# Adjacency pieces loaded from ScalarE's queue into one buffer more, with another split between two stages

## The chip, the cores and the metric

The kernel runs on one core of a Trainium2 chip. The metric is the device time in microseconds (us) of one execution. The profiles show five engines: TensorE (PE in the profile, with its weight loads as PEld), VectorE (DVE), ScalarE (ACT), GpSimd (POOL) and SyncE (SP). SP has no computation in these profiles; what it does there is issue transfers. ACT and POOL issue transfers too, between their other instructions: the load of one piece took 0.33 us to issue on SP, and 0.56 us on POOL in the kernel before. A profile is of one execution, and its span leaves out some 2 us of that execution's time, so spans of one profile and medians of several runs differ slightly. When a transfer lands is read from the profile; times to landing count from its issue.

## The reference, cut to what matters

Two layers on 4096 nodes with 512 features. The adjacency `adj` is 4096 x 4096, mostly zero.

```python
# layer 0
xw = max(sign(x), 0) @ sign(weight0).T
x  = layernorm(x + relu(adj @ xw))
# layer 1
h = x @ edge_w
e = where(adj > 0, h @ h.T, NEG_BIG)
edge_att = softmax(e, axis=1);  node_att = softmax(x @ node_w, axis=0)
x = layernorm(x + adj * (node_att * edge_att) @ (x @ weight1) + bias)
```

Layer 1 needs `adj > 0` as a mask. The kernel makes part of that mask early and in a smaller form: it loads 80 pieces of `adj` (128 rows x 1024 columns, 512 KB each), turns each into a bf16 mask on VectorE, and stores the mask (256 KB) to memory. That work has nothing to do with layer 0 or with the product h. It is only put beside them, to use their idle engines and transfer time.

## The kernel before

In layer 0, each block of 128 nodes takes 64 matmuls: the adjacency block `at` comes in two halves, each half is worked in two quarters, and each quarter is split into a high part (`hi`, a cast on ScalarE) and the rest (`lo`, a subtraction on VectorE). Both have two buffers. `premask` is called once per half.

```python
bufs = deque([pair[:, 0, :], pair[:, 1, :], single])
loaded = deque()

def premask(queue, left):
    if loaded and (len(bufs) == 1 or len(pieces) == left):
        (r, j, c), a = loaded.popleft()
        m = ...                                   # a, seen as bf16; a_ is a in the same shape
        tc.keep_in_program_order(nc.vector.tensor_scalar(m, a_, 0.0, NEG_BIG, ALU.is_le, ALU.mult))
        nc.gpsimd.dma_start(mask_d[r][:, c : c + 2, j, :], m)       # store the mask
        bufs.append(a)
    if len(pieces) > left:
        r, j, c = pieces.popleft()
        a = bufs.popleft()
        queue.dma_start(a, adj[ts(r * BG + j, P), c * W : (c + 2) * W])   # load a piece
        loaded.append(((r, j, c), a))

def aggregate(b):
    ...
    for half in range(2):
        at = stream.tile(...)                     # three buffers
        nc.sync.dma_start(at, adj_t[b, :, ts(half, HB), :])
        for q in range(2):
            ...                                   # aq: a quarter of at; tiles hi and lo, two buffers each
            nc.scalar.copy(hi, aq)
            nc.vector.tensor_sub(lo, aq, hi.bitcast(F32))
            if q == 0:
                premask(nc.gpsimd, 40)
            for c in range(QC):
                nc.tensor.matmul(acc, hi[:, c, :], xw[:, kb, :], ...)
                nc.tensor.matmul(acc, lo[:, c, :], xw[:, kb, :], ...)
    ...                                           # normalisation, rows stored
```

`tc` is a framework that orders the instructions of each engine by simulating the program, and puts in the waits. An instruction may come earlier in its engine's queue than it is written, as soon as the simulation has its inputs ready and its buffer free. `tc.keep_in_program_order(i)` forbids that for `i`: it stays behind all that was written before it for the same engine. The kernel uses it for the mask operation.

Other duties of GpSimd in layer 0: for each block, `left` and the row additions (`sums_l`, `scr`) and their stores. In the stage h (the product with `edge_w`, 56 steps of 1.72 us of matmul work) `premask(nc.sync, 0)` is called at every step after the sixth, with five buffers. The node softmax needs two reductions over partitions on GpSimd (`gmax`, `gsum`); they are written after h.

## Time and profile before

| | before |
|---|---|
| time, median of 3 | 2092.13 us (2091.34 to 2095.67) |
| layer 0 ends, h starts | 593.4 us |
| h (to the first matmul after it) | 127.2 us |
| all that follows | 1373.4 us |
| PE busy, idle from 58 to 593 | 478.4 us, 56.6 us |

The stage borders are the first starts of the matmuls of h and of the stage after it. The last row is the view by windows; the columns after the length are the busy us (and instructions) of PE, PEld, DVE, ACT and POOL, the granted clock of PE (as the profile gives it, 1.00 being its full speed), the share of time the DMA engines were busy, and GB/s:

```profile
58.00:593.00 535.00, 478.39 (x2049) 387.23 (x2048) 311.58 (x379) 148.37 (x181) 217.80 (x267) 0.95 0.68 234
```

The longest waits of GpSimd in layer 0, at loads for stored masks (total us, times, longest us):

```profile
POOL pair L274 <- DMA mask_d<-pair: 144.9, 25, 10.4
POOL single L274 <- DMA mask_d<-single: 70.5, 12, 10.0
```

### The profile page before, as it was taken

The page shows a single profiled execution, that of the slowest core. Times are in us where ns is not written, and L with a number is a line of the kernel's source. Part 1 is how long each engine was busy: PE and PEld are TensorE (multiplying, and loading weights), DVE is VectorE, ACT ScalarE, POOL GpSimd, SP SyncE. Part 2 cuts the span into 40 slices and gives each one's busy share as a digit, 9 for nine tenths or more (in the row PEclk, how much of TensorE's full clock was granted, in tenths as well). Part 3 has the DMA queues.
Part 4 walks back from the last instruction along what each step waited for, and adds up shares of the span by engine and source line. Part 5 has one row for each costly group of instructions (what it writes and reads, how often), then busy time and mean ns, then how long its engine had stood idle before and what let it go on. Part 6 is the DMA issues. An engine that isn't in the chain of part 4 may idle for free.

```text
span 2094.0 us, 18051 instructions
## 1 busy us (share of the span) xinstructions
PE 1990.7 (95%) x6108; PEld 1104.9 (53%) x6108; DVE 1377.1 (66%) x1896; ACT 673.0 (32%) x1107; POOL 526.4 (25%) x643
## 2 busy tenths in 40 slices
PE   8998887889997899999999899999999999999998
PEld 6786666678852344545555444444444444444443
DVE  7665555555566546656746877696669686887724
ACT  5332222223320156857657641112112211221100
POOL 0433433343443211111102211151114311240101
PEclk9998998999999999999999999999999999999999
DMA  8776676676537847857859897667667756766431
GB/s 298 279 271 234 210 266 218 220 286 209 195 116 274 307 173 272 316 186 262 288 205 346 297 337 259 235 241 262 230 218 264 253 195 230 265 243 222 162 107 60
DMA packets 133643, 497.70 MB, mean 238 GB/s; under 512 B 14000, under 2 KB 14000, under 8 KB 125872
## 3 DMA queue, kind: packets, MB, share of 16 engines
q0 software_dynamic: 77248, 283.15, 36.9%
q1 hardware_dynamic: 55728, 212.36, 30.2%
q10 hardware_dynamic: 576, 1.05, 0.1%
q8 instruction: 48, 0.79, 0.1%
q14 instruction: 43, 0.35, 0.0%
HBM read 376.96 MB, written 119.54 MB: 237 GB/s over the span
## 4 chain that ended last, share of the span: by engine, by line
PE 70%; DMA 14%; issue 6%; POOL 5%; DVE 4%; ACT 1%; POOLq 0%; DVEq 0%; SPq 0%; ACTq 0%
PE ps L846 37%; PE seven L660 11%; PE acc L297 5%; PE acc L296 5%; PE po L899 5%; DMA mask_d<-pair 4%; DMA more<-in_adj_dram 2%; PE pe L591 2%; DMA mask_d<-single 2%; PE pt L561 2%; PE seven L98 1%; DMA s_d<-slot 1%; POOL scr L304 1%; DVE lo L291 1%; DMA mask_d<-more 1%
## 5 line engine op out<-in xcount | busy, mean ns | idle before, releaser
L297 PE MATMUL acc<-xw,lo 128*128 128x512 f32 x960 | 389.6, 406 | 55.6 <-DVE lo L291 55.6
L846 PE MATMUL ps<-lent,lop 128*128 128x512 f32 x992 | 432.6, 592 | 0.0
L296 PE MATMUL acc<-xw,hi 128*128 128x512 f32 x960 | 388.9, 405 | 0.0
L846 PE MATMUL ps<-slot,lop 128*128 128x512 f32 x800 | 351.9, 594 | 0.0
L846 PEld LDWEIGHTS ps<-lent,lop 128*128 128x128 f32 x992 | 188.3, 190 | 236.3 <-issue 231.7
L291 DVE TENSOR_TENSOR lo<-at,hi 128x1024 fp32r<-128x1024 f32 x120 | 183.3, 1528 | 116.5 <-ACT hi L289 116.5
L846 PEld LDWEIGHTS ps<-slot,lop 128*128 128x128 f32 x800 | 152.2, 191 | 190.0 <-issue 184.4
L297 PEld LDWEIGHTS acc<-xw,lo 128*128 128x128 f32 x960 | 188.2, 196 | 103.2 <-DVE lo L291 63.7
L289 ACT CAST hi<-at 128x1024 fp32r<-128x1024 f32 x120 | 125.9, 1049 | 271.9 <-PE acc L296 264.4
L296 PEld LDWEIGHTS acc<-xw,hi 128*128 128x128 f32 x960 | 188.0, 196 | 39.1
L850 DVE TENSOR_TENSOR over<-over,ps 128x512 f32<-128x512 f32 x168 | 113.2, 678 | 96.6 <-PE ps L846 96.6
L591 PE MATMUL pe<-hT 128*128 128x512 f32 (+3 forms) x384 | 133.3, 489 | 0.0
L532 ACT ACTIVATE line<-line,nmax_c 128x512 f32<-128x512 f32 x160 | 114.8, 725 | 34.6 <-DVE nmax_c L523 34.6
L763 ACT ACTIVATE slot<-slot 128x2048 f32<-128x2048 f32 x31 | 59.3, 1913 | 201.0 <-DVE slot L760 200.9
L763 ACT ACTIVATE lent<-lent 128x2048 f32<-128x2048 f32 x33 | 62.9, 1910 | 187.4 <-DVE lent L760 184.0
L899 PE MATMUL po<-over 128*128 128x512 f32 x256 | 114.2, 593 | 3.2 <-DVE xb L908 3.2
L523 DVE CUSTOM_DVE_ANT_0 line<-lent,slot 128x512 f32<-128x512 bf16 x144 | 92.9, 686 | 35.8 <-ACT slot L601 18.8
L760 DVE CUSTOM_DVE_ANT_1 slot<-slot,line 128x2048 f32<-128x2048 f32 x31 | 73.9, 2384 | 43.3 <-DMA slot<-s_d 43.3
L151 ACT ACTIVATE rstd<-mv,eps 128x1 f32<-128x1 f32 (+1 forms) x43 | 12.6, 295 | 275.9 <-DVE mv L149 275.9
L760 DVE CUSTOM_DVE_ANT_1 lent<-lent,line 128x2048 f32<-128x2048 f32 x33 | 82.9, 2518 | 24.8 <-DMA lent<-s_d 23.5
L660 PE MATMUL seven<-hT 128*128 128x512 f32 x192 | 89.5, 593 | 0.0
L561 PEld LDWEIGHTS pt<-ident,lent 128*128 128x128 f32 x422 | 52.5, 142 | 62.2 <-issue 40.1
(195 smaller groups left out, 2654.8 us busy)
## 6 DMA issues: line engine op xcount, KB each, us to landing
at<-in_adj_t_dram SPq DMA_DIRECT2D x60, 1024.0 KB, 6.4
lop<-lop_d SPq DMA_DIRECT2D x112, 512.0 KB, 3.7
lent<-in_adj_t_dram POOLq DMA_DIRECT2D x35, 1024.0 KB, 7.1
s_d<-slot POOLq DMA_DIRECT2D x34, 1024.0 KB, 6.7
lent<-s_d POOLq DMA_DIRECT2D x33, 1024.0 KB, 7.4
slot<-s_d POOLq DMA_DIRECT2D x31, 1024.0 KB, 7.8
slot<-in_adj_t_dram POOLq DMA_DIRECT2D x29, 1024.0 KB, 7.6
lent<-in_adj_dram SPq DMA_DIRECT2D x48, 512.0 KB, 5.2
```

The costliest lines, as they stand in the source:

```text
L289: nc.scalar.copy(hi, aq)
L291: nc.vector.tensor_sub(lo, aq, hi.bitcast(F32))
L296: nc.tensor.matmul(acc, hi[:, c, :], xw[:, kb, :], start=(kb == 0), stop=False)
L297: nc.tensor.matmul(acc, lo[:, c, :], xw[:, kb, :], start=False, stop=(kb == NB - 1))
L532: nc.scalar.activation(line, line, AF.Exp, bias=nmax_c[:, b, c : c + 1], scale=-1.0, accum_out=sum_c[:, b, c : c + 1])
L591: nc.tensor.matmul(pe[:, lo * P :], hT[:, k, ts(A * BG + i, P)], hT[:, k, (B * BG + lo) * P : (B + 1) * W], start=(k == 0), stop=(k == KD ...
L660: nc.tensor.matmul(ps, left[m][:, k, q, :], right[m][:, k, :], start=(first and k == 0), stop=(k == KD // 2 - 1), skip_group_check=not first,)
L760: nc.vector._custom_dve(TENSOR_ADD_SAT, out=q, in0=q, in1=mrow.unsqueeze(1).to_broadcast([P, BG, W]), s0=0.0, s1=-HUGE)
L763: nc.scalar.activation(q, q, AF.Exp)
L846: nc.tensor.matmul(ps, lop[:, c, ts(h, P)], rop[:, c, :], start=(c == 0), stop=(c == BG - 1))
L850: nc.vector.tensor_add(total[:, m, h, :], total[:, m, h, :], ps)
L899: nc.tensor.matmul(po, (lower if k // 2 else upper)[:, k % 2, ts(i, P)], w1_s[:, k, :], start=(k == 0), stop=(k == KD - 1),)
```

## The change

Its intent: load the pieces without GpSimd, which is busy; have one buffer more, so that a load need not wait for the last store; move twelve pieces from h to layer 0, and give h seven buffers instead of five. The memory for `ends` is what the two tiles `u` had.

```diff
+        us = wp.tile([P, BG // 2, D], F32, name="us", tag="ends")
...
-                    u = wp.tile([P, D], F32, name="u", bufs=2)
+                    u = us[:, j, :]
...
-        bufs = deque([pair[:, 0, :], pair[:, 1, :], single])
+        ends = wp.tile([P, 2 * W], F32, name="ends", tag="ends")
+        bufs = deque([pair[:, 0, :], pair[:, 1, :], single, ends])
...
-            if loaded and (len(bufs) == 1 or len(pieces) == left):
+            if loaded and (len(bufs) == 2 or len(pieces) == left):
...
-                        premask(nc.gpsimd, 40)
+                        premask(nc.scalar, 28)
...
-                bufs.append(single)
+                bufs.extend((single, ends))
...
+        bufs.append(sums_l.rearrange("p n f -> p (n f)"))
-        for _ in range(4):
+        for _ in range(5):
             premask(nc.sync, 0)
...
-            if q is None and count[0] > 6:
+            if q is None and count[0] > 6 and count[0] % 3:
                 premask(nc.sync, 0)
```

## The prediction

> **What bounds the kernel now.** I read the page's tenths first: TensorE (PE) is over 90% busy nearly everywhere except in two stretches, and its granted clock dips in the same two. Then I cut the span at the stage borders with the view by windows (layer 0's blocks 60 to 593, the product h 593 to 720), and asked the waits, the chain and the timeline inside them.
>
> ```profile
> PE   8998887889997899999999899999999999999998
> PEclk9998998999999999999999999999999999999999
> 106.00:440.00 334.00, 285.46 (x1199) 229.10 (x1197) 188.37 (x225) 85.83 (x105) 123.35 (x166) 0.93 0.70 240
> 440.00:593.00 153.00, 148.82 (x660) 122.67 (x661) 89.38 (x112) 47.17 (x57) 69.31 (x73) 0.98 0.62 213
> 593.00:720.00 127.00, 104.59 (x232) 44.46 (x231) 76.42 (x105) 12.52 (x22) 45.43 (x55) 0.93 0.68 234
> 1200.00:2094.00 894.00, 883.87 (x2073) 391.99 (x2073) 640.32 (x706) 167.80 (x162) 191.80 (x201) 1.00 0.63 223
> ```
>
> After length come the busy us of PE, weight load, VectorE (DVE), ScalarE (ACT) and GpSimd (POOL), the clock, the DMA share and GB/s. The stretch 106 to 440 is where layer 0 also loads and masks adjacency pieces; from 440 on the same blocks run without them. Counting the aggregation matmuls by stretch (64 a block), 106 to 440 holds 1127, which is 17.6 blocks of 19.0 us; 440 to 593 holds 623, which is 9.7 blocks of 15.7 us. No engine is at its limit with masks; the masks cost 3.3 us a block through waiting. The last 894 us have PE 99% busy and are not touched.
>
> ```profile
> PE acc L297 <- DVE lo L291: 29.7, 9, 5.9
> DVE pair L268 <- DMA pair<-in_adj_dram: 16.1, 4, 6.1
> POOL pair L274 <- DMA mask_d<-pair: 75.8, 13, 9.5
> PE acc L297 <- DVE lo L291: 5.3, 1, 5.3
> SPq L274 <- DMA mask_d<-more: 77.3, 28, 10.7
> ```
>
> These are waits (total us, times, longest): the first three from 250 to 440, the fourth from 440 to 593, the last in h. One case out of the timeline shows how they join:
>
> ```profile
> 264.44 0.71 POOL L269 DMA_DIRECT2D mask_d<-pair  x1
> 273.25 0.56 POOL L274 DMA_DIRECT2D pair<-in_adj_dram  x1 [8.10 <-DMA mask_d<-pair]
> 279.37 0.69 DVE L268 TENSOR_SCALAR pair<-pair 128x1024 bf16<-128x1024 f32 x1 [5.37 <-DMA pair<-in_adj_dram]
> 281.31 3.40 DVE L291 TENSOR_TENSOR lo<-at,hi 128x1024 fp32r<-128x1024 f32 x1
> 284.77 0.80 PE L297 MATMUL acc<-xw,lo 128*128 128x512 f32 x1 [5.23 <-DVE lo L291]
> 285.37 0.63 PE L296 MATMUL acc<-xw,hi 128*128 128x512 f32 x1
> 285.79 0.63 PE L297 MATMUL acc<-xw,lo 128*128 128x512 f32 x1
> ```
>
> POOL stores a mask, then its queue stands 8.1 us at the next load until the store has landed, because that load reuses the stored buffer. The load lands at 279.4, VectorE has stood at its mask operation meanwhile, so the low part of the adjacency comes late, slowed to 3.40 us beside POOL's delayed adds (1.22 us is its usual undisturbed time), and PE stands 5.2 us. Afterwards matmuls start 0.425 us apart until about 290, against 0.227 us otherwise: a second cost of the same wait.
>
> [...] Issues here take 0.557 us on POOL, 0.328 us on SP, and ACT's four at the start 1.86 us, or 0.47 us each. [...]
>
> **The change part by part.** The order of the built program shows PE's sequence unchanged but for one group of four transposes; downstream of h nothing moves. "us" and "ends" merely share memory that the two u tiles had; I give that 0 us.
>
> (1) Four buffers for three, load when two are free. A load now reuses the buffer stored two calls earlier instead of one. Calls come twice a block, so the store has about 16 us to land, against its median 5 to 6 us and worst 11.3. The mask operation still comes two calls after its load, about 16 us, of which landing takes 5 (worst 9.9). Both waits should go.
>
> (2) Loads leave POOL for ACT. POOL loses 40 issues of 0.56 us and, more, some 206 us standing at line 274 from 106 to 440 (139.2 + 66.6 in the groups). Its stores, adds and the x_d stores (VectorE's scr waited 16.8 us for those) are then on time. ACT gains 52 issues of 0.47 us, 24 us in all. ACT is 26% busy in this stretch and idles for PE before most casts, and the built order puts each issue ahead of a cast or beside the transposed copy, so most of it falls into that idle time. But a quarter's turn is tight: PE needs 16 x 0.227 = 3.6 us for the other quarter, cast plus low part need 1.05 + 1.22 to 1.6 us plus hand-overs, leaving about 1 us. I charge a fifth of the 24 us, 5 us.
>
> (3) What a masked block then costs. Unmasked: 15.7 us. VectorE per block would hold four low parts of 1.39 (5.6), the normalisation 3.7 and two masks of about 0.8 (1.6): 10.9 of 15.7 us, with 4.3 us a block of idling for ACT's casts to swallow part of it. I take 16.3 us, including the odd residual stall. 106 to 440: 17.6 x (19.0 - 16.3) = 47 us saved. 60 to 106: 2.7 blocks at 17.3, 1 us saved. In the last stretch twelve more pieces bring some six blocks at perhaps 0.4 us: 2 us lost.
>
> (4) h has 28 pieces for 40, in seven buffers for five, on two of three calls. Its 112 multiplications are pairs of matmuls in the trace, 0.86 us together: 96 us, and the window is 127 us. A buffer's loop is load 5.8 + mask 0.7 + store issue 0.7 + store 4.7 to 6, about 12.5 us; five buffers allow one piece per 2.5 us, and 36 pieces in the last 100 us (2.8 us each) say that this loop sets the pace, not PE. Seven buffers allow 1.8 us, and a call in three left out asks for one every 2.6 us. A load is then five calls, 13 us, ahead of its mask. So VectorE no longer stands for it and PE's own 96 us should show; with starting and group borders (POOL's t waits) I take 100: 27 us saved.
>
> Sum: 47 + 1 - 2 - 5 + 27 = 68 us; 2092 - 68 = 2024 us.
>
> **The rivals.** First, DMA becomes the bound. For it: per block the traffic stays about 19.0 x 240 = 4.56 MB, so at 16.3 us it asks 280 GB/s, and the share 0.70 grows by 19.0/16.3 to about 0.82. Against it: 0 to 60 ran at 304 GB/s and share 0.88, 60 to 106 at 262 with little waiting, h reaches 400 in single slices, and the adjacency blocks are loaded up to three halves ahead. If it binds at about 265 GB/s, a block takes 17.2 us, layer 0 saves some 30 instead of 46, and the time is about 2040.
>
> Second, ACT takes over POOL's wait: a load standing on ACT for a late store holds every cast, and PE is only 1 us behind. For it: strict order, stores still from POOL behind its adds, up to 11 us to land[...]. Against it: two calls of room. If a third of the loads stood 3 us with PE exposed, 52 us or the whole layer-0 gain would go: about 2070. I give this one in twelve.
>
> Third, the masks' mere presence on VectorE costs what they cost now, beside POOL, so layer 0 keeps 18 us a block and only h gains: about 2045. Against it, PE's waits for low parts fall from 47.4 us to 5.3 us between the two stretches, and the traced cases begin with a load that was late.
>
> Fourth, h turns VectorE-bound: per group of 24 us it has ten adds of 0.68, three subtractions of 1.22 and seven masks of 0.7 to 1, some 17 us. It is too little to bind, but a bad order could leave h at 108: 2032.
>
> **Range and chances.** Everything working, with masked blocks at 15.8 and h at 97, gives 2006. DMA binding together with a poorer h (108) gives 2048; part of the second rival adds to that. I take 2006 to 2056. The 2% line is at 2050, which needs more than a third of the expected gain to fail: faster 0.88, same 0.11, slower 0.01.
>
> **What would show it.** POOL's wait for stored masks, 206 us, should nearly vanish and not come up on ACT: ACT's waits before the adjacency loads should total under 15 us. VectorE's waits for loaded pieces, 45 us in layer 0 and 44 in h, should fall under 10 each. PE's wait for low parts from 60 on, 55.6 us, should fall to 10 to 15, its clock in layer 0 rise from 0.93 to 0.97 or more, and h end about 100 us after it starts. Layer 0 should end near 552, h near 652, and the rest keep its length of 1374 us within 3 us. I am wrong if ACT shows waits of several us before casts, if the adjacency blocks' landing grows from 6.4 us to over 9 with PE waiting for them, or if the couples' stage after h grows because its first operands or masks come in another order.

## The result, and the profile after

The changed kernel took 2064.11 us (median of 4, 2061.74 to 2067.15) beside 2091.74 us (2091.29 to 2095.67) for the kernel before. The ratio is 0.9865, with a 95% interval from 0.9845 to 0.9885. A ratio here is the mean time of one kernel's fast runs over that of the other's in the same rounds, so it is not quite the ratio of the medians. The change gained some 28 us, less than half of what was forecast, and the time lies 8 us outside the stated range.

| | before | after | forecast for after |
|---|---|---|---|
| h starts | 593.4 | 577.4 | 552 |
| h | 127.2 | 106.6 | 100 |
| the rest | 1373.4 | 1375.6 | 1374 |
| span | 2094.0 | 2059.6 | |

So layer 0 gained 16 us instead of 41, h gained 20.6 instead of 27, and the rest lost 2.2 us. That makes 34.4 us between the two profiled executions, against 28 between the medians: the one before, at 2096.0 us, was above its kernel's median, and the one after, at 2061.7, the fastest of four. In the windows of the kernel after, layer 0 has 37.2 us without PE (519.00 less 481.76), and the clock is no better than it was:

```profile
58.00:577.00 519.00, 481.76 (x2046) 387.17 (x2045) 316.77 (x390) 147.08 (x181) 223.82 (x241) 0.95 0.74 261
577.00:683.60 106.60, 98.70 (x233) 43.52 (x232) 68.25 (x95) 12.42 (x22) 35.79 (x43) 0.98 0.53 187
```

The waits of the kernel after (total us, times, longest us): the first four in layer 0, the last three in h.

```profile
PE acc L299 <- ACT hi L292: 26.2, 12, 4.1
PE acc L300 <- DVE lo L294: 10.9, 14, 2.2
ACT hi L292 <- DMA mask_d<-ends: 74.5, 9, 9.9
ACT hi L292 <- DMA mask_d<-pair: 20.0, 5, 4.9
POOL gsum L403 <- ACT hT L124: 10.8, 1, 10.8
DVE more L271 <- DMA more<-in_adj_dram: 9.9, 3, 4.8
PE seven L98 <- DVE hT L119: 7.8, 2, 5.0
```

GpSimd no longer waits for stored masks in layer 0; that was 215 us before. ScalarE does now, 94.5 us, in front of its casts, and TensorE waits for the casts. A cast reads nothing from `mask_d`. What waited is the load that stands ahead of the cast in ScalarE's queue. One case, from the timeline of the kernel after, put together from VectorE, GpSimd and ScalarE (ACTq is ScalarE's queue issuing a transfer):

```profile
345.36 1.77 DVE L271 TENSOR_SCALAR ends<-ends 128x1024 bf16<-128x1024 f32 x1
...
346.55 1.18 POOL L318 TENSOR_TENSOR sums_l<-sums_l,xb 128x256 f32<-128x256 f32 x1
349.35 0.77 POOL L323 DMA_DIRECT2D lop_d<-sums_l  x1
350.68 0.71 POOL L272 DMA_DIRECT2D mask_d<-ends  x1
...
349.00 1.05 ACT L292 CAST hi<-at 128x1024 fp32r<-128x1024 f32 x1 [2.92 <-PE acc L299]
358.83 0.33 ACTq L277 DMA_DIRECT2D ends<-in_adj_dram  x1
359.26 1.04 ACT L292 CAST hi<-at 128x1024 fp32r<-128x1024 f32 x1 [9.21 <-DMA mask_d<-ends]
```

The mask is done at 347.1. GpSimd still has its additions and two stores ahead of the mask's store, which goes out at 350.68 and lands 8.1 us later, at 358.8. ScalarE's load of the very same buffer has stood since 350.05, and behind it the cast. The chain of waits goes on from there to the low part (360.34) and the matmuls, which come back at 361.62 and start 0.43 us apart until 367.5, then 0.23 us apart.

Why does the load stand there? The prediction counted two calls, some 16 us, between a mask and the load that reuses its buffer. That is how the source is written. But in the order of the built program, the scheduler had moved each load up. Here is the order on ScalarE; the corresponding mask on VectorE stands between the two halves of the same block:

```
L292 TensorCopy hi<-at                  [waits for DMA, PE]
L277 DMACopy ends<-in_adj_dram          [waits for the store of ends, VectorE, ...]
L292 TensorCopy hi<-at
L329 TensorCopy x1T<-pt
L277 DMACopy pair<-in_adj_dram          [waits for the store of pair, VectorE, ...]
```

The trace has ScalarE's part in the same order, at 323.41 to 325.33 us for one. The load of `ends` follows the store of `ends`, not the store two calls later. It seems that in the simulation the store had landed by this place; its times were not read. On the chip it had not. The buffer more gave no slack: it was turned into an earlier place in the queue. The experiments test this reading.

### The profile page after: what moved, and what is told of

The parts are those of the page before. It is cut to its first block, busy times and chain, and to the rows that moved or that the text cites.

```text
span 2059.6 us, 18124 instructions
## 1 busy us (share of the span) xinstructions
PE 1989.2 (97%) x6108; PEld 1104.0 (54%) x6108; DVE 1370.2 (67%) x1896; ACT 673.0 (33%) x1107; POOL 522.6 (25%) x603
## 4 chain that ended last, share of the span: by engine, by line
PE 70%; DMA 9%; issue 7%; POOL 6%; DVE 4%; ACT 2%; ACTq 0%; POOLq 0%; SPq 0%; DVEq 0%
PE ps L850 37%; PE seven L664 11%; PE po L903 5%; DMA mask_d<-ends 4%; PE seven L98 4%; PE acc L300 3%; PE acc L299 3%; PE pe L595 2%; POOL scr L307 2%; PE pt L565 2%; DMA s_d<-slot 1%; DMA mask_d<-pair 1%; ACT hi L292 1%; DVE lo L294 1%; PE acc L236 1%
## 5 line engine op out<-in xcount | busy, mean ns | idle before, releaser
L294 DVE TENSOR_TENSOR lo<-at,hi 128x1024 fp32r<-128x1024 f32 x120 | 155.5, 1297 | 148.1 <-ACT hi L292 148.0
L595 PEld LDWEIGHTS pe<-hT 128*128 128x128 f32 x384 | 64.6, 191 | 37.9 <-issue 31.0
```

The source lines that it names most:

```text
L595: nc.tensor.matmul(pe[:, lo * P :], hT[:, k, ts(A * BG + i, P)], hT[:, k, (B * BG + lo) * P : (B + 1) * W], start=(k == 0), stop=(k == KD ...
```

## The experiments

Theory A: a load moved up in the queue of an engine with other work holds that work (9.2 us in the case above); the queue and the place cause nearly all of layer 0's loss. Rivals: traffic or VectorE's masks set the pace (B), the loads delay the blocks from wherever they are issued (C), the fourth buffer is what helps (D). Theory E covers h: GpSimd stood at a reduction, with mask stores behind it. Nine kernels were run. All outputs are right.

| run | what it changes | median (range), us | ratio to before (95%) | h starts | h |
|---|---|---|---|---|---|
| e1_pinned | after, loads kept in place | 1997.10 (1996.28 to 1998.08) | 0.9541 (0.9524 to 0.9559) | 513.8 | 107.2 |
| e2_sp | after, loads from SP | 1996.64 (1995.04 to 1997.76) | 0.9536 (0.9515 to 0.9558) | 512.7 | 107.4 |
| e3_pool4 | after, loads from GpSimd | 2080.78 (2079.78 to 2083.95) | 0.9944 (0.9923 to 0.9964) | 594.3 | 108.0 |
| e4_act3 | after, three buffers | 2061.83 (2052.07 to 2065.44) | 0.9839 (0.9804 to 0.9875) | 577.4 | 106.8 |
| e5_reduce_late | after, reductions behind h | 2049.27 (2038.83 to 2058.06) | 0.9788 (0.9749 to 0.9827) | 575.9 | 96.9 |
| e7_best | e1 and e5 together | 1986.67 (1984.52 to 1988.35) | 0.9493 (0.9473 to 0.9514) | 513.3 | 96.8 |
| e8_pinned3 | e1 with three buffers | 2052.27 (2049.22 to 2059.13) | 0.9812 (0.9786 to 0.9837) | 566.7 | 107.1 |
| e9_before_sp | before, loads from SP | 2014.72 (2010.48 to 2019.34) | 0.9628 (0.9604 to 0.9652) | 511.9 | 124.6 |
| e10_pinned40 | e7 with the split 40 and 40 | 1997.39 (1995.44 to 1999.92) | 0.9545 (0.9525 to 0.9566) | 513.7 | 107.6 |

### e1_pinned: the loads kept at their written place

```diff
-                queue.dma_start(a, adj[ts(r * BG + j, P), c * W : (c + 2) * W])
+                load = queue.dma_start(a, adj[ts(r * BG + j, P), c * W : (c + 2) * W])
+                if queue is nc.scalar:
+                    tc.keep_in_program_order(load)
```

> The changed kernel, with each adjacency load of layer 0 kept at its written place on ScalarE, two calls behind the mask of its buffer, where the scheduler had moved it up to just behind that buffer's own store. Theory A (the moved-up load stands in ScalarE's strict queue and holds the casts): ScalarE's waits for stored masks (94.5 us before its casts in the changed kernel) fall under 10 us, PE's waits in layer 0 from 37 us to under 12, layer 0 ends near 552 instead of 577, total about 2038 us (2030 to 2046). Rival B (DMA traffic or VectorE's masks set the pace of a masked block): the waits move to the adjacency blocks or to VectorE and the total stays at 2058 to 2066.

It took 1997.10 us, 67 us less than the changed kernel. ScalarE's waits for stored masks are gone altogether. In the waits of this kernel in layer 0, the cast waits only for PE, and PE once for a low part:

```profile
ACT hi L294 <- PE acc L301: 256.4, 117, 6.3
PE acc L302 <- DVE lo L296: 1.8, 1, 1.8
```

In its timeline, the same buffer's mask, store and next load now lie like this:

```profile
331.81 0.69 DVE L271 TENSOR_SCALAR single<-single 128x1024 bf16<-128x1024 f32 x1
332.80 0.73 POOL L272 DMA_DIRECT2D mask_d<-single  x1 [5.34 <-DVE single L271]
344.63 0.33 ACTq L277 DMA_DIRECT2D single<-in_adj_dram  x1
```

The load comes 11.8 us after the store went out, and neither it nor the cast behind it waits. Not a computation, a transfer, a buffer or a byte differs from the changed kernel; only the order does, and with it the wait instructions that the framework puts in (36 instead of 60 at this line on ScalarE's queue). That shows theory A and rules out B: from 58 to 512 this kernel moves 297 GB/s at a DMA share of 0.84, against 266 at 0.76 after, and PE is busy 451.2 of 454 us.

The size, though, was missed: 26 us were expected, 67 measured. The expectation took off only PE's waits. Here are the windows of e7_best, which has the same layer 0:

```profile
58.00:513.00 455.00, 452.43 (x2051) 373.60 (x2050) 313.91 (x391) 150.12 (x181) 221.05 (x241) 1.00 0.84 298
513.00:610.00 97.00, 96.89 (x232) 43.13 (x231) 67.18 (x95) 12.42 (x22) 35.50 (x43) 1.00 0.62 206
```

Layer 0 is 64 us shorter than in the kernel after (519 less 455). PE's idle time fell from 37.2 to 2.6 us, which is 34.7 us. Its busy time for the same matmuls fell from 481.8 to 452.4 us, which is 29.3 us: the clock went from 0.95 to 1.00. The waits of PE cost almost as much again in slow matmuls after them. This is no fixed rate: in the kernel before, PE was idle 54.0 us longer than here (56.6 less 2.6) and busy only 26.0 us longer (478.4 less 452.4).

### e2_sp: the loads from SP

```diff
-                        premask(nc.scalar, 28)
+                        premask(nc.sync, 28)
```

> The changed kernel, with the layer 0 loads issued from SP instead of ScalarE; the scheduler still moves them up. Theory A: no compute engine stands behind a waiting load any more; SP stands instead, and the three adjacency block buffers (about 24 us of work) cover it: layer 0 ends near 555, total about 2040 us (2032 to 2048). Rival B (traffic): no gain, 2058 to 2066. Rival C (SP's own waits delay the adjacency blocks as much as ScalarE's delayed the casts): 2058 or more, with ScalarE's casts waiting for at.

It took 1996.64 us, the same as e1_pinned. Here the loads are still moved up, and they still wait, more than ever. SP's waits from 58 to 545 us, the first 32 us of h among them, include:

```profile
SPq L277 <- DMA mask_d<-ends: 122.4, 14, 9.9
SPq L277 <- DMA mask_d<-pair: 113.5, 14, 10.8
```

With `single` that is 273 us, of which 256 us lie in layer 0, and TensorE lost 1.1 us there in waits for low parts. SP has nothing to compute, and the adjacency blocks behind the loads have three buffers. So rival C falls as well. Here a load that waits is harmless; the engine it stands on decides. The size was missed for the same reason as in e1_pinned.

### e3_pool4: the loads back on GpSimd, four buffers kept

```diff
-                        premask(nc.scalar, 28)
+                        premask(nc.gpsimd, 28)
```

> The changed kernel, with the layer 0 loads back on GpSimd: four buffers and 52 pieces, only the queue undone. In its built order each load stands right behind the store of its own buffer. Theory A (the queue matters, a buffer more does not, as the scheduler turns it into an earlier place and not into slack): GpSimd stands over 250 us in layer 0 for stored masks, layer 0 ends at 590 or later, total 2075 to 2095 us. Rival D (the fourth buffer was what helped): total within 8 us of the changed kernel, 2056 to 2072.

It took 2080.78 us. Layer 0 ends where it ended before (594.3 against 593.4), though twelve more pieces are in it, and GpSimd's waits for stored masks from 58 to 595 are back, at 242.7 us (215.4 before; over 250 were expected):

```profile
POOL ends L277 <- DMA mask_d<-ends: 98.8, 11, 10.3
POOL pair L277 <- DMA mask_d<-pair: 90.2, 24, 7.1
POOL single L277 <- DMA mask_d<-single: 53.7, 12, 6.0
```

In its built order, the load of a buffer stands directly behind that buffer's own store. The gain over the kernel before comes from h, 108.0 us instead of 127.2; the rest is longer by 2 us in the profile, as in the kernel after.

### e4_act3: the changed kernel with three buffers

```diff
-        bufs = deque([pair[:, 0, :], pair[:, 1, :], single, ends])
+        bufs = deque([pair[:, 0, :], pair[:, 1, :], single])
-            if loaded and (len(bufs) == 2 or len(pieces) == left):
+            if loaded and (len(bufs) == room[0] or len(pieces) == left):   # room[0] is 1 here, 2 in h
```

> The changed kernel with three buffers in layer 0 instead of four, loads on ScalarE, left where the scheduler puts them. Theory A (without the kept place the fourth buffer buys nothing, since each load stands right behind its own buffer's store either way): ScalarE's waits for stored masks stay at 70 to 130 us, layer 0 ends at 572 to 590, total 2058 to 2078. Rival D (the fourth buffer does help as written): layer 0 ends after 595, total over 2082.

It took 2061.83 us, the changed kernel's time. ScalarE's waits for stored masks sum to 68 us (58.8 and 9.5), just under the 70 to 130 expected; the last matmul of layer 0's blocks starts at 576.7 in both kernels. As the change was written, the fourth buffer bought nothing measurable. Rival D falls.

### e8_pinned3: loads kept in place, three buffers

The edits of e1_pinned and e4_act3 together.

> Loads kept at their written place on ScalarE, but three buffers in layer 0 instead of four (h unchanged with seven): a load then reuses a buffer masked one call, 7.6 us, before it instead of two. Theory A' (the fourth buffer is worth something once the order lets it be slack): the store, issued 1 to 5 us after the mask and landing in 4 to 8, is late for part of the loads; ScalarE waits 60 to 150 us, total 2020 to 2065. Rival G (the place in the queue was everything): ScalarE waits under 15 us, total under 2002.

It took 2052.27 us: with the order kept, three buffers cost 55 us against four. The slack is one call here, and part of the stores do not land within it. From the timeline of this kernel, GpSimd and ScalarE:

```profile
345.10 0.71 POOL L273 DMA_DIRECT2D mask_d<-pair  x1
...
352.62 0.33 ACTq L278 DMA_DIRECT2D pair<-in_adj_dram  x1
353.05 1.04 ACT L295 CAST hi<-at 128x1024 fp32r<-128x1024 f32 x1 [7.52 <-DMA xb<-in_x_dram]
```

The profile names the load of `xb` as the releaser, and so do its 76 us of such waits. That name is wrong. The load of `xb` went out at 348.81 and landed 5.0 us later, at 353.8, after the waiting load was already out. The store went out at 345.10 and landed 7.5 us later, at 352.6, which is when the load went. In the other six waits that I followed, the store's landing fits in the same way. So the fourth buffer is worth its place, but only with the order kept: the 7.6 us from a mask to the load are too little where the store goes out some us after the mask and lands in up to 8.7 us (this kernel's layer 0), and 15 us were enough in e1_pinned, where it landed in up to 9.8.

### e9_before_sp: one word in the kernel before

```diff
-                        premask(nc.gpsimd, 40)
+                        premask(nc.sync, 40)
```

> The kernel before with one word changed: its layer 0 loads are issued from SP instead of GpSimd; three buffers, 40 pieces, h as before. Theory A: layer 0's whole loss came from an engine with other duties standing at a load; SP has slack of three block buffers, so layer 0 ends at 515 to 530 instead of 593, h keeps 127 us, total 2014 to 2032. Rival C (with three buffers SP stands so long that blocks come late): ScalarE's casts wait for at, total over 2050.

It took 2014.72 us, 49 us less than the changed kernel, with three buffers and the old split. Layer 0 ends at 511.9 us, earlier than the 515 to 530 expected and as with four buffers and the loads in place. h keeps 124.6 us. So the whole of layer 0's loss in the kernel before came from having the loads on GpSimd. The move also takes 40 issues of 0.56 us, 22 us, off GpSimd; no run kept its loads there but in their written place, so that part is not separated from the 215 us of standing.

### e5_reduce_late: the reductions behind h

```diff
-    nc.gpsimd.partition_all_reduce(gmax, nmax, P, bass_isa.ReduceOp.max)
+    tc.keep_in_program_order(nc.gpsimd.partition_all_reduce(gmax, nmax, P, bass_isa.ReduceOp.max))
```

`gsum` depends on `gmax` and follows it.

> The changed kernel, with the two reductions over partitions for the node attention (gmax, gsum) kept behind h on GpSimd, instead of between the mask stores of h. Theory E (GpSimd stood 10.8 us for gsum's input in h, its stores came late, so loads and then VectorE's masks): PE's wait in h (7.8 us) goes, h shrinks from 106 to about 99 us, total about 2057 us (2053 to 2061). Rival F (h is bound by GpSimd's t, or by VectorE, anyway): h stays at 104 or more and the total at 2061 to 2068.

It took 2049.27 us, a little better than expected, but its four runs are spread over 19 us; layer 0, left as in the changed kernel, may vary with the landing of stores, which I did not test. The profile is clear for h: 96.9 us instead of 106.6, and no wait of PE in it. In the kernel after, the scheduler had put `gsum` among the mask stores of h. GpSimd stood 10.8 us for its input, which itself stood behind a copy on ScalarE; the stores behind it were late, then the loads, then VectorE's masks (9.9 and 3.9 us), then the results that TensorE waited for. It is the same pattern as in layer 0, on another engine. Rival F falls.

### e7_best: both mends

The edits of e1_pinned and e5_reduce_late together, timed in five rounds.

> Both mends together: loads kept at their written place on ScalarE, reductions kept behind h on GpSimd. If the two costs lie in different stages and are independent, their gains add: layer 0 ends near 513 as with the first alone, h takes 96 us as with the second alone instead of 107, total 1997 - 10.5 = 1986.5 us (1984 to 1990). If h's gain of the second was luck of that run's spread (2038.8 to 2058.1), 1993 to 1998.

It took 1986.67 us, where 1986.5 was expected: the gains add. This version beats both kernels, by 5.1% against before. In its windows, shown above, PE is busy 452.4 of 455 us in layer 0 and 96.9 of 97 in h. Within these two stages nothing is left but TensorE's own work.

### e10_pinned40: the split undone

```diff
-                        premask(nc.scalar, 28)
+                        premask(nc.scalar, 40)
-            if q is None and count[0] > 6 and count[0] % 3:
+            if q is None and count[0] > 6:
```

on top of e7_best.

> Both mends, with the split of pieces undone: 40 of 80 in layer 0 and 40 in h at every call after the sixth, seven buffers in h. My step 4 (a buffer's loop is about 12.5 us, seven buffers allow a piece every 1.8 us, asked for every 1.72): h about 100 to 106 us instead of 96, layer 0 still ends near 513, total 1990 to 1997. Rival H (the split was needed, the transfers cannot follow): h over 112 us, total over 2002.

It took 1997.39 us, at the upper edge of what was expected (0.4 us over), with h at 107.6 us instead of 106 at most. Moving twelve pieces to layer 0 is worth 10.7 us: layer 0 takes them for nothing (513.3 against 513.7), while h with 40 pieces makes VectorE stand for loads and PE for VectorE (7.2 us).

## Why the prediction was wrong, point by point

**What bounds the kernel now: right, with one detail wrong.** e9_before_sp confirms that the loads standing on GpSimd cost layer 0 its time. But the load did not wait for the store of one call earlier. In the kernel before, too, it had been moved up behind the store of its own buffer. The prediction's case, a store of `pair` and then a load into `pair`, cannot tell, since `pair` is two buffers. The next one on GpSimd can, since as written a load into `pair` would follow the store of `single`:

```profile
275.47 0.75 POOL L269 DMA_DIRECT2D mask_d<-single  x1 [1.66 <-issue]
280.53 0.56 POOL L274 DMA_DIRECT2D single<-in_adj_dram  x1 [4.31 <-DMA mask_d<-single]
```

Had I matched the buffers there, I would have seen the scheduler's habit. (The "worst 11.3" us for a store is from a view that mixes in later loads of the mask; the stores alone took at most 10.6.)

**Step (1) failed, and it decided the result.** It said that a load reuses the buffer stored two calls earlier, "so the store has about 16 us to land", and that "both waits should go". The built order gave the store no such room. GpSimd's wait of 215 us became ScalarE's of 94.5 us. With the 16 us given for real (e1_pinned), the waits go, as the step says. VectorE's waits for loaded pieces in layer 0 did fall, from 45 us to none that the profile lists.

**Step (2) was half right.** GpSimd was freed. I charged 5 us for ScalarE's issues, at 0.47 us each; an issue took 0.33 us, and in e1_pinned, where all 52 are on ScalarE, PE waits 1.8 us for low parts in the whole of layer 0. The charge was at most that.

**Step (3) was sized wrongly in the other direction.** A masked block was put at 16.3 us. Without the waits it takes 15.2 us (455 us for 30 blocks, masked or not), which is TensorE's own pace. I had taken 15.7 us from the stretch without masks as a floor, though that stretch still held a wait of 5.3 us and a clock of 0.98. So had step (1) held, the time would have been 1997 and not 2024: too low a gain here hid the size of the error in (1). There is also a slip in its sum: 2.7 blocks from 17.3 to 16.3 us save 2.7 us, not 1.

**Step (4) had the right mechanism and a size off.** h was to take 100 us and took 106.6. The starting and border losses that I allowed for, 4 us, were 10.6 us over the 96 us of matmuls, and e5_reduce_late shows all but 0.9 us of them to be the reduction on GpSimd: 96.9 us without it. VectorE's waits for pieces in h fell from 44 us to 13.8, not under 10. I had not looked for the reduction, though the profile before showed GpSimd idle for 10.2 us ahead of `gsum` there.

**The rivals.** The second, ScalarE taking over GpSimd's wait, is what happened, at 2064 us where I had put it at about 2070. I gave it one chance in twelve, because of "two calls of room" that were not there. The sign of being wrong that I had named for it, ScalarE waiting several us before casts, is what the profile shows. The first (transfers) is refuted by e1_pinned at 297 GB/s, the third (the masks' presence) by the same run. The fourth is half right: h was longer than forecast, but GpSimd's order did it, not VectorE's load.

**Range and chances.** The upper end, 2056, stood for two things going wrong at once (2048) and a part of the second rival on top. That rival alone was enough. By the 2% line the change counts as the same (ratio 0.9865), to which I had given 0.11. What stays open is the 2.2 us that the rest took longer in the profile after (1375.6 us, against 1373.5 in e1_pinned and 1374.4 in e7_best); no run explains it. e4_act3, which differs only in layer 0, had 1373.6, so it may be no more than the spread of single profiles.

## What to carry to other kernels

When a load reuses a buffer, find its place in the built order of the engine that issues it, and match it by buffer with the store it waits for: a scheduler that takes the store for landed can spend a new buffer on an earlier place and not on slack, as here. The slack has to cover the late stores: in layer 0 of the kernel after, the mask stores landed in 2.5 us at the least, 4.0 in the median and 9.1 at most. Put loads that may wait on an engine that has nothing to compute, or keep them where they are written: the same transfers took 67 us less from SP than from ScalarE, with 273 us of waits for stored masks on SP from 58 to 545 us, beside 1.1 us of TensorE's waits for low parts. And count more for a wait of TensorE than its length: here each us of idle time in layer 0 came with 0.5 us (before) to 0.8 us (after) of slower matmuls. Short waits had such matmuls behind them too: in the kernel after, idle stretches of 1.20 us before the start at 150.43 and 0.76 us before the one at 151.69 were followed by starts 0.43 us apart from 153.12 to 156.11, beside 0.23 us up to 148.85.
